# Correlation channels as a fourth term of each convolution product, in place of joins by row group

## The chip, the cores and the metric

The kernel runs on one core of one Trainium2 chip. The metric is the device time of one execution in microseconds (us); before the change the median of three runs is 2604.48 us (2602.58 to 2604.71). Besides, one execution was profiled. In the text PE is the tensor engine, DVE the vector engine, ACT the scalar engine, POOL the GpSimd engine and SP the sync engine, which here issues nearly all DMAs.

## The reference

The input is `x` of 8 images, 768 channels, 32 by 32 pixels, in 32-bit floats. Two layers with a residual follow each other:

```
x = x + attention(groupnorm(x))
x = x + conv(groupnorm(x))
```

The attention has 12 heads of 64 over 1024 tokens. Its scores are made from the variances of v and k alone, `softmax(var_v * var_k^T * scale) @ v`, and a projection by `W_proj` follows.

The second layer is what the change is about:

```
norm   = sqrt(sum(feature**2, channels));  feat_n = feature / max(norm, eps)
corr   = 28 maps: sum over channels of feat_n shifted by (r, c) times feat_n
out    = conv_w @ concat(feature, corr) + conv_b      # a 1x1 convolution, 768 + 28 -> 768
```

So each output value is a sum over 768 feature channels and 28 correlation channels of the same token.

## The kernel before, in words

**Products of seven.** All large matrix products are done by a scheme of Strassen's kind: both operands are cut into two by two blocks, sums of blocks are formed, and seven block products, numbered p = 1 to 7, are added into the four output blocks. For the convolution of one image the output channels are six tiles of 128 (two halves by three groups g = 0 to 2) and the tokens are two halves of 512, so there are 3 x 7 = 21 products, each of three channel tiles of 128. A product is one call chain of `halves` (line 350): every 128 by 512 matmul is issued as two column halves of 64. The products gather in PSUM banks: x for p = 1, 6, 7, 4, y for 5, 3, z for 2 (`BANK`, `FIRST`, `LAST`); x has two buffers, y and z share two. `Wide.take` adds a finished partial sum to the output with DVE.

**Correlation.** `Corr.gram` (line 1151) multiplies windows of the image with turned copies of it, the result is copied out of PSUM into a `win` tile and sent to DRAM, `diagonals`, `scale` and `gather` bring the wanted sums back as rows, and `product` writes them to `cs`: 28 rows, for both token halves and their difference. The weights lie in `wcorr_sb`. Both are tiles of 128 partitions. Four of the seven products, p = 2, 3, 7, 4, are the last of an output block, and the correlation channels are added with those: 12 of the 21 products per image (`Conv.more`).

**Joins.** Before the change `begin` leaves such a product's bank open (`stop=False`); once four or two products are held, `join` (line 1057) issues one matmul of 28 rows by 128 columns for each, the n-th at partitions 32n, so that they use different row groups of the array. For this `wcorr_sb` and `cs` are copied by DMA to partitions 32, 64 and 96. For images 0 to 5 the joins of an image hold 4, 4, 2 and 2 products, for image 6 two each, the last of them at the end of the next projection. When the first join has four, product (0, 2) goes to a bank of its own (`apart`). In the last image the correlation isn't joined to products: `corr` (line 1344) makes 12 products of it alone, by twos on two row groups, and DVE adds them.

**Order of the work.** A planner written out in Python (`Clock`) fixes the order of the instructions of each queue at build time. It has a price for each unit: `T_US` 2.58 for a product, `CORR_US` 1.2 for a join, `STEP_US` 1.73 for an attention step, `EXP` 1.07 for an exponential. `work_off` puts runs of four attention steps of image b (`av`, line 800) between units of the convolution of image b-1, whenever the plan has enough exponentials ahead. A unit waits in the plan for keys such as ("cs", b). `conv_order` gives the order of the 21 products, and with it the order in which SP loads the weight tiles `wt`, seven buffers deep.

**Other places touched.** `keep_warm` issues matmuls of an identity at the start, 31 of them before the first norm (`WARM`). `set_aside` copies three tiles of the features and two of the output before the last projection, with ACT (line 229, tiles `held`), into buffers of the exponentials' pool; the two products that stay over from image 6 use them later. In the last image the turned copies (`turn`) are made by ACT, in other images by POOL; the copies of the gram into `win` are DVE's in all images (line 167 is the helper of all DVE operations).

Of the kernel before, what the change touches and what calls it, by code (L numbers as in the profile page):

```python
# [8 lines left out]
ALU = mybir.AluOpType  # L9
# [43 lines left out]
HELD = 12  # L53
TAIL = 0.0
EXP, SUM, STEP_US = 1.07, 1.15, 1.73
KV_US, T_US, CORR_US = 1.93, 2.58, 1.2
GRAM_US = 1.4
WARM, BRIDGE = 31, (3, 7)

# [12 lines left out]
ORDER = (1, 5, 6, 3, 7, 4, 2)  # L72
QUADS = PAIR[:10] + ((0, 2),) + PAIR[10:12] + ((1, 2), (2, 5), (2, 1)) + SINGLE[2:]
FOUR = P // 4
LOWS = (
# [6 lines left out]
def conv_order(b):  # L82

    return QUADS if b < NB - 2 else (PAIR[:-2] if b == NB - 2 else PAIR) + SINGLE

# [87 lines left out]
def two_layers(ctx, tc, x, wkv, wproj, bproj, wconv, wcorr, bconv, out):  # L173
# [181 lines left out]
    class Banks:  # L355
# [7 lines left out]

        def product(self, g, p, us, width, pairs, taken, home=None):
            self.close(*self.begin(g, p, width, pairs, home=home), us, taken)

        def begin(self, g, p, width, pairs, stop=True, between=None, apart=False, home=None):
            bank = BANK[p]
            if apart:
                t = other([P, width], f"{bank}{g}")  # L370
                for k, (lhsT, rhs) in enumerate(pairs):
                    halves(t, lhsT, rhs, start=k == 0, stop=False, skip_group_check=True)
                return ("apart", g), t
# [12 lines left out]
            clock.pass_time(max(self.free.get(slot, 0.0) - clock.now, 0.0))  # L386
            for k, (lhsT, rhs) in enumerate(pairs):
                halves(
                    t, lhsT, rhs, start=p in FIRST and k == 0, stop=stop and k == len(pairs) - 1, skip_group_check=True
                )  # L390
                if between and k == 0:
                    between()
            return slot, t
# [81 lines left out]
    def load_corr_weights():  # L475

        zero = cs[0:NROW, 0, 0:PAD]
        for r in rows:
            nc.sync.dma_start(out=r[:, 0:PAD], in_=zero)
            nc.sync.dma_start(out=r[:, PAD + N : ROW], in_=zero)  # L480
        for line, step in enumerate(STEP):
            for j in (1, 2, 3):
                n, k = CHANNELS.index(step * j), 3 * line + j - 1
                nc.sync.dma_start(out=wcorr_sb[n : n + 1, :, :], in_=wcorr[k : k + 1, :, :])
                nc.sync.dma_start(out=wcorr_sb[NS + n : NS + n + 1, :, :], in_=wcorr[NS + k : NS + k + 1, :, :])
        nc.sync.dma_start(out=wcorr_sb[2 * NS : NCH, :, :], in_=wcorr[2 * NS : NCH, :, :])
        for n in range(1, 4):
            nc.sync.dma_start(out=wcorr_sb[n * FOUR : n * FOUR + NCH, :, :], in_=wcorr_sb[0:NCH, :, :])

# [447 lines left out]
    class Attention:  # L937
# [32 lines left out]
        def exp_work(self, pair, t):  # L970
# [6 lines left out]
            def job():  # L977
                pair.exponentials(t)
                self.made += 1
                self.exp_at = clock.act  # L980

# [47 lines left out]
    class Wide:  # L1029
        def __init__(self, kind, name, acc, bias, operand, finished, more=None):  # L1030
            self.kind, self.name, self.acc, self.bias = kind, name, acc, bias
            self.operand, self.finished, self.more, self.held = operand, finished, more, []
            self.joined, self.home = [], None

# [3 lines left out]
        def unit(self, g, p, between=None):  # L1038
# [3 lines left out]
            more = self.more(g, p) if self.more else None  # L1042
            if more is None:
                banks.product(g, p, T_US, HF, pairs, taken, self.home if g == 2 else None)
            else:
                apart = (g, p) == (0, 2) and self.joined[:1] == [4]
                self.held.append((*banks.begin(g, p, HF, pairs, stop=False, between=between, apart=apart), taken, *more))
                if len(self.held) == (self.joined[0] if self.joined else 2):
                    self.joined = self.joined[1:]
                    self.join()  # L1050
            t_stream.fill()

        def join(self):

            for n, (slot, t, taken, i, tokens) in enumerate(self.held):
                at = slice(n * FOUR, n * FOUR + NCH)
                nc.tensor.matmul(  # L1057
                    t, lhsT=wcorr_sb[at, i, :], rhs=cs[at, tokens, :], start=False, stop=True, skip_group_check=True
                )
            for slot, t, taken, i, tokens in self.held:  # L1060
                banks.close(slot, t, T_US + CORR_US, taken)
            self.held = []

# [55 lines left out]
    class Corr:  # L1119
# [18 lines left out]
        def gram(self, t):  # L1138
# [22 lines left out]
            def out():  # L1161
                win = wins[t % 2 if t < MT - 1 else 2]
                vector.tensor_copy(win[:, :n], ps[:, :n])
                for side in range(2):
# [58 lines left out]
        def gather(self):  # L1223
# [15 lines left out]
            def product():  # L1239
                vector.tensor_tensor(u, u, v, ALU.mult)  # L1240
                vector.tensor_tensor(cs[0:NCH, 2, :], cs[0:NCH, 0, :], cs[0:NCH, 1, :], ALU.subtract)
                for n in range(1, 4):
                    nc.sync.dma_start(out=cs[n * FOUR : n * FOUR + NCH, :, :], in_=cs[0:NCH, :, :])
                later.after_dve(6.0, lambda: ready.add(("cs", b)))

            later.after(18.0, product)

    class Conv:


        def __init__(self, b, f, acc, after):
            self.b, self.f, self.acc, self.after = b, f, acc, after
            self.early, self.then = False, None
            self.turn = False
            self.apart = [] if b < NB - 1 else [(i, hf) for i in (0, 3, 1, 4, 2, 5) for hf in range(2)]
# [11 lines left out]
        def start(self):  # L1267
# [8 lines left out]
            )  # L1276
            self.wide.joined = [4, 4] if self.b < NB - 2 else []
            ready.add(("acc", self.b))
# [18 lines left out]
        def units(self):  # L1297
            b, held, sizes = self.b, 0, [4, 4] if self.b < NB - 2 else []
            need = {7: (("third", b),), 4: (("fourth", b),)}
            out = []  # L1300
            for g, p in conv_order(b):
                keys, us = need.get(p, ()), T_US
                if self.more(g, p):
                    keys, held = keys + (("cs", b),), held + 1
                    if held == (sizes[0] if sizes else 2):
                        us, held, sizes = us + CORR_US, 0, sizes[1:]
                out.append((us, keys, lambda g=g, p=p: self.unit(g, p)))
# [7 lines left out]
        def set_aside(self):  # L1315

            first, second, third = [expool.tile([P, 2, HF], F32, tag="ex", name=f"held{n}") for n in range(3)]
            self.high = [first[:, 0, :], first[:, 1, :], second[:, 0, :]]
            self.low = {g: third[:, g, :] for g in range(2)}
            for k in range(JH):  # L1320
                act_copy(0.55, self.high[k], self.f[:, JH + k, :HF])
            for g in range(2):
                act_copy(0.55, self.low[g], self.acc[:, g, :HF])

# [7 lines left out]
        def corr_units(self):  # L1332
            return [
                (CORR_US, (("cs", self.b),), lambda n=n: self.corr(self.apart[n : n + 2])) for n in range(0, len(self.apart), 2)
            ]
# [38 lines left out]
    def work_off(rest, attention=None, beside=()):  # L1374
        while rest or (attention and not attention.over()):
            if attention and not attention.over():
                clock.feed_act()
                if attention.can_run():
                    next_to(beside)
                    attention.run()  # L1380
                    next_to(beside)
                    continue
                if ("v", attention.b, 1) in ready and sum(r[0] for r in rest) <= TAIL:
                    clock.pass_time(0.5)
                    continue
# [132 lines left out]
    for b in range(NB + 1):  # L1518
# [8 lines left out]
        if b:  # L1527
# [17 lines left out]
            if b < NB:  # L1545
# [69 lines left out]
```

## Time and profile before

| what | value |
|---|---|
| median of three runs | 2604.48 us |
| the profiled execution | 2601.92 us |
| its span in the profile | 2599.4 us |
| PE busy | 2586.6 us, 14776 instructions |
| DVE busy | 1609.8 us |
| ACT busy | 1368.6 us |
| POOL busy | 416.0 us |
| matmuls from `cs` and `wcorr_sb`, 28x128 form | 192 instructions (84, 42, 42 and 12, 12) |
| DMA copies `cs<-cs` | 24, of 168 KB |

A line of a group reads: source line, engine, operation, output tile and input tiles, shape, count; then busy time, mean ns of one, and idle time before. `128*64` on PE means 128 active rows and 64 active columns. Durations of PE overlap, as matmuls are pipelined, so the pace is read from starts. Every matmul call in 32-bit floats shows as two instructions in the trace.

### The profile page before, as it was taken

The page shows a single profiled execution, that of the slowest core. Times are in us where ns is not written, and L with a number is a line of the kernel's source. Part 1 is how long each engine was busy: PE and PEld are TensorE (multiplying, and loading weights), DVE is VectorE, ACT ScalarE, POOL GpSimd, SP SyncE. Part 2 cuts the span into 40 slices and gives each one's busy share as a digit, 9 for nine tenths or more (in the row PEclk, how much of TensorE's full clock was granted, in tenths as well). Part 3 has the DMA queues.
Part 4 walks back from the last instruction along what each step waited for, and adds up shares of the span by engine and source line. Part 5 has one row for each costly group of instructions (what it writes and reads, how often), then busy time and mean ns, then how long its engine had stood idle before and what let it go on. Part 6 is the DMA issues. An engine that isn't in the chain of part 4 may idle for free.

```text
span 2599.4 us, 40526 instructions
## 1 busy us (share of the span) xinstructions
PE 2586.6 (100%) x14776; PEld 1351.1 (52%) x14776; DVE 1609.8 (62%) x4118; ACT 1368.6 (53%) x1841; POOL 416.0 (16%) x444
## 2 busy tenths in 40 slices
PE   9999999999999999999999999999999999999999
PEld 5654465434664347643476435764356643575333
DVE  6868735775347853488535885357853578535764
ACT  1497179701797017970189701896018960199500
POOL 4320130004300043000330013300133001330000
PEclk9999999999999999999999999999999999999999
DMA  8866366355563655636556365463654636545323
GB/s 295 291 222 216 105 206 206 102 200 168 175 206 96 203 169 173 202 105 200 171 170 201 121 200 169 156 205 118 206 170 144 207 123 205 187 125 169 114 91 106
DMA packets 324716, 448.16 MB, mean 172 GB/s; under 512 B 59810, under 2 KB 245522, under 8 KB 324518
## 3 DMA queue, kind: packets, MB, share of 16 engines
q1 hardware_dynamic: 322454, 442.24, 53.0%
q10 hardware_dynamic: 2064, 3.34, 0.4%
q8 instruction: 117, 1.92, 0.3%
q14 instruction: 81, 0.66, 0.1%
HBM read 376.70 MB, written 64.40 MB: 170 GB/s over the span
## 4 chain that ended last, share of the span: by engine, by line
PE 96%; DVE 1%; DMA 1%; ACT 0%; issue 0%; POOL 0%; SPq 0%; DVEq 0%; ACTq 0%; POOLq 0%
PE x L350 34%; PE av L800 25%; PE y L350 17%; PE z L350 9%; PE own L350 5%; PE gr L1151 3%; PE den L831 1%; PE den L887 1%; PE y L1057 1%; PE z L1057 1%; ACT ex L774 0%; DMA bc<-vdr 0%; DVE acc L167 0%; DMA xn<-in_x_dram 0%; DVE bn L167 0%
## 5 line engine op out<-in xcount | busy, mean ns | idle before, releaser
L774 ACT ACTIVATE ex<-bc,nk 128x1024 f32<-128x1024 f32 x768 | 827.5, 1137 | 403.9 <-DMA bc<-vdr 206.1
L800 PE MATMUL av<-ex,v 128*64 128x512 f32 x3072 | 693.5, 593 | 1.2 <-ACT ex L774 1.1
L800 PEld LDWEIGHTS av<-ex,v 128*64 128x64 f32 x3072 | 332.2, 137 | 318.4 <-issue 199.3
L784 ACT ACTIVATE junk<-bk,vm 128x1024 bf16<-128x1024 f32 x368 | 420.4, 1142 | 28.8 <-DMA bk<-kdr 19.1
L167 DVE TENSOR_TENSOR acc<-acc,ex 128x1024 f32<-128x1024 f32 x300 | 345.2, 1211 | 0.8 <-ACT ex L774 0.8
L229 ACT COPY kp<-x 128x384 f32<-128x384 f32 x28 | 13.3, 478 | 524.1 <-PE x L350 515.4
L350 PE MATMUL y<-kv,s 128*64 128x384 f32 x1488 | 265.3, 487 | 0.3 <-POOL s L636 0.3
L350 PE MATMUL x<-kv,xn 128*64 128x384 f32 x1512 | 259.5, 486 | 0.0
L350 PE MATMUL x<-kv,s 128*64 128x384 f32 x1488 | 256.4, 486 | 0.0
L350 PEld LDWEIGHTS x<-kv,xn 128*64 128x64 f32 x1512 | 139.5, 137 | 104.0 <-issue 83.8
L350 PEld LDWEIGHTS x<-kv,s 128*64 128x64 f32 x1488 | 142.6, 137 | 93.3 <-issue 72.7
L350 PEld LDWEIGHTS y<-kv,s 128*64 128x64 f32 x1488 | 137.0, 137 | 89.9 <-issue 72.4
L530 POOL TENSOR_TENSOR rstda<-vea,neghalf 128x1 f32<-128x1 f32 x8 | 4.8, 595 | 958.6 <-DVE vea L167 958.6
L1136 POOL TENSOR_TENSOR turn<-f,ones 128x384 f32<-128x384 f32 x112 | 110.9, 1010 | 242.7 <-PE gr L1151 165.7
L350 PE MATMUL z<-kv,xn 128*64 128x384 f32 x768 | 133.7, 486 | 0.0
L350 PE MATMUL x<-f,wt 128*64 128x512 f32 x504 | 118.3, 592 | 0.0
L167 DVE TENSOR_TENSOR v<-y,v 128x128 f32<-128x128 f32 x180 | 40.9, 282 | 122.2 <-PE y L350 122.2
L636 POOL TENSOR_TENSOR s<-xn 128x384 f32<-128x384 f32 x64 | 65.6, 1035 | 304.3 <-PE x L350 190.0
L167 DVE BATCH_NORM_STATS2 vbn<-v 128x6 f32<-128x64 f32 x720 | 101.6, 209 | 0.0
L350 PEld LDWEIGHTS z<-kv,xn 128*64 128x64 f32 x768 | 74.9, 137 | 47.3 <-issue 36.6
L167 DVE SCALAR_TENSOR_TENSOR xn<-x,bconv_sb,xn 128x512 f32<-128x512 f32 x63 | 46.3, 745 | 80.8 <-PE x L350 79.7
L1151 PEld LDWEIGHTS gr<-f,turn 128*64 128x64 f32 x1344 | 87.8, 136 | 13.0 <-issue 4.8
(202 smaller groups left out, 3132.3 us busy)
## 6 DMA issues: line engine op xcount, KB each, us to landing
kv<-kvs SPq DMA_DIRECT2D x124, 576.0 KB
kv<-in_wkv_dram SPq DMA_DIRECT2D x95, 576.0 KB
bc<-vdr SPq DMA_DIRECT2D x96, 512.0 KB
f<-in_x_dram SPq DMA_DIRECT2D x48, 512.0 KB
bk<-kdr SPq DMA_DIRECT2D x46, 512.0 KB
x1d<-f SPq DMA_DIRECT2D x42, 512.0 KB
xn<-x1d SPq DMA_DIRECT2D x42, 512.0 KB
out_dram<-xn SPq DMA_DIRECT2D x82, 256.0 KB
```

The source lines that it names most:

```text
L167: return getattr(self.engine, name)(*args, **kw)
L229: nc.scalar.copy(to, at)
L350: nc.tensor.matmul(out[at], lhsT=lhsT[:, at], rhs=rhs, start=start, stop=stop, **kw)
L636: nc.gpsimd.tensor_tensor(self.sums[g][:, 0], a[g][2], a[g][3], ALU.add)
L774: nc.scalar.activation(ex, self.bc[e], AF.Exp, scale=self.kv.nk[self.half][:, h, t : t + 1])
L784: nc.scalar.activation(junk, self.bk[e], AF.Exp, scale=self.kv.m2[self.half][:, h, t : t + 1], accum_out=self.sums[:, e, t : t + 1],)
L800: nc.tensor.matmul(self.av[hf][e * HD : (e + 1) * HD, :], lhsT=self.vt[:, t, e, :], rhs=exs[e][:, hf * HF : (hf + 1) * HF], start=t == 0, ...
L831: nc.tensor.matmul(den[at * 32 : (at + 1) * 32, :], lhsT=ones[:, 0:32], rhs=self.acc[e][:, hf * HF : (hf + 1) * HF], start=True, stop=True,)
L887: nc.tensor.matmul(den[e * HD : (e + 1) * HD, :], lhsT=ones, rhs=self.acc[e][:, at], start=True, stop=True)
L1057: nc.tensor.matmul(t, lhsT=wcorr_sb[at, i, :], rhs=cs[at, tokens, :], start=False, stop=True, skip_group_check=True)
L1136: nc.gpsimd.tensor_tensor(to[:, :, side], half, windows(ones, ones.ap[0], (0, J), (HW, 4), (1, HW)), ALU.mult)
L1151: nc.tensor.matmul(ps[side * HD : (side + 1) * HD, :n].rearrange("p (y x) -> p y x", x=WIDE), lhsT=block[:, j, side, :], rhs=image[:, 4 * ...
```

## The change

The held products and the joins go. A product that takes a correlation term gets a fourth pair, `wcorr_sb` and `cs` on all 128 rows (rows 28 and up are zero), issued by `halves` like the other three, and is closed at once. The copies to partitions 32, 64 and 96 go, and with them the time that the plan allows for them. The 12 separate products of the last image are made in the same form, by fours. The order of the 21 products is one list (`SPACED`) for all images but for the two products that stay over in image 6. `CORR_US` becomes 0.43 and stands for one correlation product. In the last image ACT copies the gram into `win`, and the product that makes `cs` is placed 12 instead of 18 us after its loads. `set_aside` copies with POOL, by a multiplication with ones, at the end of the list of units and after the last exponential. The warm-up has 42 matmuls instead of 31. `TAIL`, which is 0.0, goes with its branch.

```
-WARM, BRIDGE = 31, (3, 7)
+WARM, BRIDGE = 42, (3, 7)
-KV_US, T_US, CORR_US = 1.93, 2.58, 1.2
+KV_US, T_US, CORR_US = 1.93, 2.58, 0.43
-QUADS = PAIR[:10] + ((0, 2),) + PAIR[10:12] + ((1, 2), (2, 5), (2, 1)) + SINGLE[2:]
-FOUR = P // 4
+SPACED = PAIR[:11] + ((0, 2), (2, 1), (1, 4), (2, 5), (2, 6), (2, 3), (1, 2), (2, 7), (2, 2), (2, 4))
...
 def conv_order(b):
-    return QUADS if b < NB - 2 else (PAIR[:-2] if b == NB - 2 else PAIR) + SINGLE
+    return tuple(q for q in SPACED if b != NB - 2 or q not in ((0, 2), (1, 2)))
...
-        for n in range(1, 4):
-            nc.sync.dma_start(out=wcorr_sb[n * FOUR : n * FOUR + NCH, :, :], in_=wcorr_sb[0:NCH, :, :])
...
+                if self.made == HP * MT:
+                    ready.add(("made", self.b))
...
             more = self.more(g, p) if self.more else None
-            if more is None:
-                banks.product(g, p, T_US, HF, pairs, taken, self.home if g == 2 else None)
-            else:
-                apart = (g, p) == (0, 2) and self.joined[:1] == [4]
-                self.held.append((*banks.begin(g, p, HF, pairs, stop=False, between=between, apart=apart), taken, *more))
-                if len(self.held) == (self.joined[0] if self.joined else 2):
-                    self.joined = self.joined[1:]
-                    self.join()
+            us = T_US
+            if more:
+                i, tokens = more
+                pairs.append((wcorr_sb[:, i, :], cs[:, tokens, :]))
+                us += CORR_US
+            banks.product(g, p, us, HF, pairs, taken, between, self.home if g == 2 else None)
             t_stream.fill()
-
-        def join(self):
-            for n, (slot, t, taken, i, tokens) in enumerate(self.held):
-                at = slice(n * FOUR, n * FOUR + NCH)
-                nc.tensor.matmul(
-                    t, lhsT=wcorr_sb[at, i, :], rhs=cs[at, tokens, :], start=False, stop=True, skip_group_check=True
-                )
-            for slot, t, taken, i, tokens in self.held:
-                banks.close(slot, t, T_US + CORR_US, taken)
-            self.held = []
...
-                vector.tensor_copy(win[:, :n], ps[:, :n])
+                if b < NB - 1:
+                    vector.tensor_copy(win[:, :n], ps[:, :n])
+                else:
+                    act_copy(0.3, win[:, :n], ps[:, :n])
...
-                for n in range(1, 4):
-                    nc.sync.dma_start(out=cs[n * FOUR : n * FOUR + NCH, :, :], in_=cs[0:NCH, :, :])
-                later.after_dve(6.0, lambda: ready.add(("cs", b)))
-            later.after(18.0, product)
+                later.after_dve(1.5, lambda: ready.add(("cs", b)))
+            later.after(18.0 if b < NB - 1 else 12.0, product)
...
+            def copy(to, at):
+                one = windows(ones, ones.ap[0], (0, HF // HD), (1, HD))
+                to, at = [a.rearrange("p (n d) -> p n d", d=HD) for a in (to, at)]
+                nc.gpsimd.tensor_tensor(to, at, one, ALU.mult)
             for k in range(JH):
-                act_copy(0.55, self.high[k], self.f[:, JH + k, :HF])
+                copy(self.high[k], self.f[:, JH + k, :HF])
             for g in range(2):
-                act_copy(0.55, self.low[g], self.acc[:, g, :HF])
+                copy(self.low[g], self.acc[:, g, :HF])
...
-            self.turn = not self.turn
-            av = None if self.turn else two_banks(f"av{self.b}_{parts[0][0]}")
-            for n, (i, hf) in enumerate(parts):
-                at = slice(n * FOUR, n * FOUR + NCH)
-                ps = other([P, HF], f"cc{self.b}_{i}_{hf}") if av is None else av[n]
-                nc.tensor.matmul(ps, lhsT=wcorr_sb[at, i, :], rhs=cs[at, hf, :], start=True, stop=True)
-                later.after(1.0, lambda i=i, hf=hf, ps=ps: self.corr_taken(i, hf, ps))
+            some = [other([P, HF], f"cc{self.b}_{i}_{hf}") for i, hf in parts[:2]]
+            for n, (ps, (i, hf)) in enumerate(zip(some + two_banks(f"av{self.b}_{parts[0][0]}"), parts)):
+                halves(ps, wcorr_sb[:, i, :], cs[:, hf, :])
+                later.after((n + 1) * CORR_US + 0.1, lambda i=i, hf=hf, ps=ps: self.corr_taken(i, hf, ps))
...
-                    rest.insert(len(rest) - 3, (0.0, (), conv.set_aside))
+                    rest.append((0.0, (("made", b),), conv.set_aside))
...
-                rest += [first, start] + units[:2] + grams + units[2:18]
-                for n, unit in enumerate(units[18:]):
-                    rest += parts[2 * n : 2 * n + 2] + [unit]
+                rest += [first, start] + units[:2] + grams + units[2:17]
+                for n, unit in enumerate(units[17:]):
+                    rest += parts[n : n + 1] + [unit]
```

More of the change, by code (lines that the diff above doesn't have):

```diff
@@ L53 @@
 HELD = 12
-TAIL = 0.0
 EXP, SUM, STEP_US = 1.07, 1.15, 1.73
-KV_US, T_US, CORR_US = 1.93, 2.58, 1.2
+KV_US, T_US, CORR_US = 1.93, 2.58, 0.43
 GRAM_US = 1.4
-WARM, BRIDGE = 31, (3, 7)
+WARM, BRIDGE = 42, (3, 7)
 BANK = {1: "x", 6: "x", 7: "x", 4: "x", 5: "y", 3: "y", 2: "z"}
@@ L362, in finish, with product, begin @@
                 self.free[slot] = job()
-        def product(self, g, p, us, width, pairs, taken, home=None):
-            self.close(*self.begin(g, p, width, pairs, home=home), us, taken)
-        def begin(self, g, p, width, pairs, stop=True, between=None, apart=False, home=None):
+        def product(self, g, p, us, width, pairs, taken, between=None, home=None):
+            self.close(*self.begin(g, p, width, pairs, between, home), us, taken)
+        def begin(self, g, p, width, pairs, between=None, home=None):
             bank = BANK[p]
[L369 to L373, printed above, removed]
             of = "x" if bank == "x" else "y"
@@ L388, in begin @@
                 halves(
-                    t, lhsT, rhs, start=p in FIRST and k == 0, stop=stop and k == len(pairs) - 1, skip_group_check=True
+                    t, lhsT, rhs, start=p in FIRST and k == 0, stop=k == len(pairs) - 1, skip_group_check=True
                 )
@@ L1031, in __init__ @@
             self.kind, self.name, self.acc, self.bias = kind, name, acc, bias
-            self.operand, self.finished, self.more, self.held = operand, finished, more, []
-            self.joined, self.home = [], None
+            self.operand, self.finished, self.more, self.home = operand, finished, more, None
         def place(self, i, hf):
@@ L1253, in __init__ @@
             self.early, self.then = False, None
-            self.turn = False
             self.apart = [] if b < NB - 1 else [(i, hf) for i in (0, 3, 1, 4, 2, 5) for hf in range(2)]
@@ L1276, in start @@
             )
-            self.wide.joined = [4, 4] if self.b < NB - 2 else []
             ready.add(("acc", self.b))
@@ L1297, in units @@
         def units(self):
-            b, held, sizes = self.b, 0, [4, 4] if self.b < NB - 2 else []
+            b = self.b
             need = {7: (("third", b),), 4: (("fourth", b),)}
@@ L1303, in units @@
                 if self.more(g, p):
-                    keys, held = keys + (("cs", b),), held + 1
-                    if held == (sizes[0] if sizes else 2):
-                        us, held, sizes = us + CORR_US, 0, sizes[1:]
+                    keys, us = keys + (("cs", b),), us + CORR_US
                 out.append((us, keys, lambda g=g, p=p: self.unit(g, p)))
@@ L1333, in corr_units @@
             return [
-                (CORR_US, (("cs", self.b),), lambda n=n: self.corr(self.apart[n : n + 2])) for n in range(0, len(self.apart), 2)
+                (4 * CORR_US, (("cs", self.b),), lambda n=n: self.corr(self.apart[n : n + 4]))
+                for n in range(0, len(self.apart), 4)
             ]
         def corr(self, parts):
-            self.turn = not self.turn
-            av = None if self.turn else two_banks(f"av{self.b}_{parts[0][0]}")
-            for n, (i, hf) in enumerate(parts):
-                at = slice(n * FOUR, n * FOUR + NCH)
-                ps = other([P, HF], f"cc{self.b}_{i}_{hf}") if av is None else av[n]
-                nc.tensor.matmul(ps, lhsT=wcorr_sb[at, i, :], rhs=cs[at, hf, :], start=True, stop=True)
-                later.after(1.0, lambda i=i, hf=hf, ps=ps: self.corr_taken(i, hf, ps))
+            some = [other([P, HF], f"cc{self.b}_{i}_{hf}") for i, hf in parts[:2]]
+            for n, (ps, (i, hf)) in enumerate(zip(some + two_banks(f"av{self.b}_{parts[0][0]}"), parts)):
+                halves(ps, wcorr_sb[:, i, :], cs[:, hf, :])
+                later.after((n + 1) * CORR_US + 0.1, lambda i=i, hf=hf, ps=ps: self.corr_taken(i, hf, ps))
         def corr_taken(self, i, hf, ps):
@@ L1381, in work_off @@
                     next_to(beside)
-                    continue
-                if ("v", attention.b, 1) in ready and sum(r[0] for r in rest) <= TAIL:
-                    clock.pass_time(0.5)
                     continue
```

## The prediction

> **What bounds the kernel now.** I read the first page of the profile first, then the waits of PE, then the order of time on PE. Three lines of the page (span, busy time by engine, the chain that ended last):
>
> ```profile
> span 2599.4 us, 40526 instructions
> PE 2586.6 (100%) x14776; PEld 1351.1 (52%) x14776; DVE 1609.8 (62%) x4118; ACT 1368.6 (53%) x1841; POOL 416.0 (16%) x444
> PE x L350 34%; PE av L800 25%; PE y L350 17%; PE z L350 9%; PE own L350 5%; PE gr L1151 3%; PE den L831 1%; PE den L887 1%; PE y L1057 1%; PE z L1057 1%; ACT ex L774 0%; DMA bc<-vdr 0%; DVE acc L167 0%; DMA xn<-in_x_dram 0%; DVE bn L167 0%
> ```
>
> PE is busy for all but 12.8 us, and the chain is PE for 96%. A busy PE need not run at its peak, so I asked what it waits for. The complete list of PE's waits has only these of any size:
>
> ```profile
> PE pma L350 <- DVE mva L167: 2.8, 1, 2.8
> PE gr L1151 <- DVE win L167: 2.0, 4, 1.0
> PE warm L419 <- POOL ident masks.py:199: 1.6, 1, 1.6
> PE av L800 <- ACT ex L774: 1.1, 3, 0.6
> ```
>
> So nothing that the change does on DVE, ACT, POOL or the DMA queues can win much; what it does to the number and form of PE's instructions counts in full. The granted clock is 1.00 in every stretch that I asked for. One stretch of PE in order of time (start, duration, then line, tiles, shape, count), in the convolution of the first image:
>
> ```profile
> 441.22 5.47 PE L350 MATMUL y<-t1f,wt 128*64 128x512 f32 x24
> 446.37 5.47 PE L350 MATMUL x<-t2f,wt 128*64 128x512 f32 x24
> ...
> 473.20 2.90 PE L350 MATMUL y<-f,wt 128*64 128x512 f32 x12
> 476.03 0.69 PE L1057 MATMUL y<-cs,wcorr_sb 28*128 28x512 f32 x1
> 476.04 0.70 PE L1057 MATMUL x<-cs,wcorr_sb 28*128 28x512 f32 x2
> 476.05 1.10 PE L1057 MATMUL y<-cs,wcorr_sb 28*128 28x512 f32 x2
> 476.57 0.59 PE L1057 MATMUL x<-cs,wcorr_sb 28*128 28x512 f32 x2
> 476.58 0.59 PE L1057 MATMUL y<-cs,wcorr_sb 28*128 28x512 f32 x1
> 477.10 1.06 PE L831 MATMUL den<-acc,ones 128*32 128x512 f32 x8
> ```
>
> Starts tell the true pace, since durations overlap. Each matmul call is two instructions in the trace. Twenty-four instructions of the 128x64 form take 446.37 - 441.22 = 5.15 us: 0.2146 each, 0.858 us for one call of `halves` (two column halves, four instructions), 2.575 us for a product of three. A join of four products is the eight instructions at 476.03: the four row groups start within 20 ns of each other and run side by side. From 473.20 the product should end at 475.775; the next work starts at 477.10, so this join costs 1.33 us for four products.
>
> **The change, part by part.**
>
> *The correlation as a fourth pair of each product.* Per image there are 12 products that take a correlation term (p = 2, 3, 7, 4 by three groups), so 96 in eight images. The two programs' instruction lists agree: 96 calls of 28x128 form go (192 instructions, lines 1057 and 1344), 192 calls of 128x64 form come (384 instructions, in `halves`). No other PE work changes but 11 warm-up calls. Added: 96 x 0.858 = 82.4 us. The nearest rows are those of the same shape; the quickest pace is 0.2146 a instruction, the slowest group of L350 at 128x512 has 0.2256 with its waits, so the ends are 82.4 and 86.6. I take 82.4.
>
> *The joins go.* I measured all 33 places as above (next start, less start of the last product, less 2.575). Twelve joins of four cost 15.8 us (1.33 each, one 1.17), eighteen joins of two cost 21.0 us (1.16 mostly, 1.31 where the next tile follows differently), the three groups of four at L1344 in the last image 2.56, 2.07 and 2.07, together 6.7. Sum 43.4 us. Eight joins stand before `den` products of line 831, whose 128x32 form brings a switch of its own (the last start before it is 0.523 us ahead instead of 0.422), which stays: 0 to 0.8 us comes back, I take 0.5. So PE's own work grows by 82.4 - 43.4 + 0.5 = 39.5.
>
> *A rule beside the row.* The rows show four row groups in 1.07 us from first start to the next work, where four full-height products will need 3.43. The Trainium skill, "TensorEngine Tiling (Array Packing)", section Overview, gives a contraction of at most 32 rows an up to fourfold gain from packing, which speaks against undoing the packing; its section Key Properties adds that a change of the tiling mode drains the engine. By full packing without any drain each join would be one pass of 0.858 (an estimate from that page), the old cost 36 x 0.858 = 30.9 us and the loss 51.5; the trace's 1.16 to 1.33 includes what the switch costs, and the sum goes by it.
>
> *Copies and waits ahead of the joins.* 27 DMAs (`cs<-cs` 24, `wcorr_sb` 3) go, and `cs` counts as ready 1.5 us instead of 6.0 us after its product. They cost SP about 0.83 us of issue each, off the path; PE nowhere waits for `cs` (largest in the waits: 0.2 us at a weight load). Worth 0; at most that 0.2.
>
> *The other order of products.* The same 21 products. What could cost is a bank used again before DVE took it: in the new order three places have one product between two uses of a bank, (0,4) to (2,1), (2,5) to (2,3), (2,7) to (2,4). One product is 2.575 us, with a correlation 3.43; a take is 0.69 to 0.75 us on DVE. The old order even has (2,6) straight behind (2,1) in one bank, and PE's list has no wait on it. Worth 0 while DVE's queue holds less than 1.7 us of other work; beyond that see rival B.
>
> *The planner's price.* CORR_US 0.43 is half of the 0.858 a product takes, so PE comes 5 us behind the plan per image. DVE, ACT and SP are then early against PE, not late; 0. If something placed too early blocks its queue, it is rival B again.
>
> *Warm-up.* 11 more calls before the first norm. In order of time the warm calls start 0.111 us apart per instruction from 5.4 us on, so 22 add 2.45 us; PE waits 2.83 us there for `mva`. Hidden; 0, and at most 0.2 if that gap shrinks.
>
> *Aside copies from ACT to POOL, last attention.* ACT and PE in order of time:
>
> ```profile
> 2440.86 1.65 ACT L229 COPY held<-f 128x512 f32<-128x512 f32 x3
> 2447.36 1.14 ACT L229 COPY held<-xn 128x512 f32<-128x512 f32 x2 [4.85 <-PE av L800]
> 2448.40 4.51 ACT L774 ACTIVATE ex<-bc,nk 128x1024 f32<-128x1024 f32 x4
> ...
> 2445.44 3.60 PE L800 MATMUL av<-ex,v 128*64 128x512 f32 x16
> 2449.60 3.15 PE L800 MATMUL av<-ex,v 128*64 128x512 f32 x10 [0.56 <-ACT ex L774]
> 2452.97 1.50 PE L800 MATMUL av<-ex,v 128*64 128x512 f32 x5 [0.22 <-ACT ex L774]
> ```
>
> The copies of `held<-xn` wait 4.85 us on ACT for a buffer, four exponentials stand behind them, and PE starves. From 2445.44 PE has 32 instructions of av (6.87), a product (2.575) and a join (1.16), so 2456.0; it gets to the next work at 2458.46: 2.4 us lost. With the copies on POOL and behind the last exponential, this goes: 0 to -2.4, I take -2.1, since the page shows nothing else late there. On POOL each copy is about 1.35 us (1010 ns for 384 columns, scaled), five are 6.7. Queued behind them on POOL is only the next norm's `rstdb`, 60 us later. On SP the reload of `f` columns 3 to 5 (first at 2458) must wait for them, with weight loads behind it; seven weight tiles are ahead, 18 us of PE. 0; without that cover some 2 us.
>
> *Last image's gram copied by ACT.* The four waits of the second list, here in place:
>
> ```profile
> 2529.94 1.58 PE L1151 MATMUL gr<-f_last,turn 128*64 128x133 f32 x24 [0.98 <-DVE win L167]
> 2531.95 2.94 PE L1151 MATMUL gr<-f_last,turn 128*64 128x133 f32 x48 [0.43 <-DVE win L167]
> 2535.12 2.94 PE L1151 MATMUL gr<-f_last,turn 128*64 128x133 f32 x48 [0.23 <-DVE win L167]
> 2538.44 1.01 PE L1151 MATMUL gr<-f_last,turn 128*64 128x76 f32 x24 [0.38 <-DVE win L167]
> ```
>
> DVE's copies queued there behind 0.6 us operations. On ACT a gram brings two turns (0.93) and a copy of about 0.3, so 1.25 us against 1.45 of PE. But a turn now stands behind a copy that waits for PE and for the DMA that empties the window. -2.0 to +2; I take -1.3.
>
> *The correlation product 6 us sooner in the last image.* It is placed 12 us after its loads are begun, not 18. Those issues ran 2561.3 to 2566.2, so they have 7 us to land; the product ran at 2576.6. The first corr unit is also one product earlier. PE did not wait there; 0. At the tail the last two units are the same two, and the 3.9 us from PE's last start to the end stay.
>
> **Sum.** +39.0 +0.5 (den switches) -2.1 -1.3 = +36.1 us. Against the profiled execution's own 2601.92 us (span 2599.4 and 2.5 around it) that is 2638.0. That execution lies 2.6 us under the median of the three timed runs, 2604.48, which gives 2640.6; I forecast 2640.5, +1.4%.
>
> **The rivals.**
>
> A. *ACT becomes the bound of the grams*: a turn held up by window copies, about 1.0 us for each of 8 grams instead of the gain: +36.1 +1.3 +8 = +45, 2650. For it: the window copies of DVE did wait for the DMA (1.0 to 1.6 us, four times). Against: 1.25 against 1.45 us.
>
> B. *Banks or blocked queues make PE wait*: three places per image in seven images, each for one sum of DVE's attention work (1.16 us) = 24: 2665. For it: those sums come in pairs and fours on DVE. Against: no such wait in the old order, which has a closer pair.
>
> C. *The other side, faster*: a correlation product costs what the planner says, 0.43 us: 41.3 - 43.4 + 0.5 - 3.4 = -5, 2599.5. For it: only that constant. Against: every row of that shape, av included, stands at 0.858. It decides below (43.4 + 2.9) / 96 = 0.48 us a product.
>
> D. *The joins cost more than their place shows*, since four banks held open and four takes at once press DVE: another 6 us back, 2634. For it: DVE waits 88 us for joins. Against: PE's list has no wait for a take.
>
> **How the numbers follow.** The forecast's own terms end at 34.6 (43.4 off 82.4, no switch, both gains whole) and 46.2 (86.6 less 43.4, 0.8, no gain, 2 lost in the grams): 2639 to 2651. Forecast 0.78, D 0.06, A 0.06, B 0.06, C 0.02, and 0.02 that it is some lesser mix near no change. The range 2631 to 2651 holds the forecast, A, and D with the 2 to 3 us by which runs differ; left out are C, B's full price and the mix. Within 0.2% (5.2 us, about what a measurement of this kernel can tell from no change) 0.01; faster 0.02; slower 0.97.
>
> **What would show it.** Right: PE busy time up by some 35 to 37 us with the share still 100%; groups with `cs,wcorr_sb` at 128*64, 384 instructions of about 593 ns, 12 products an image, each 3.43 us from start to start; no 28-row form; no `PE av <- ACT ex` in the last attention; the DVE `win` waits gone or replaced by ACT `win`. Wrong: new waits of PE on DVE `xn` (B) or on ACT `turn` or `win` (A), or a start-to-start time of a cs group well under 0.8 us (C).

## The result, and the profile after

The changed kernel takes 2641.43 us (median of four runs, 2639.12 to 2644.45) against 2603.53 us for the kernel before (median of four, 2601.29 to 2604.71; three of them are the runs told of ahead): a ratio of 1.0148, 95% interval 1.0136 to 1.0160. It is slower by 38 us. The forecast was 2640.5. The four runs of the changed kernel lie in two pairs, 2639.1 and 2639.4 us at a mean granted clock of 1.00 and 2643.4 and 2644.5 at 0.999; the profile is of the first.

The page of the changed kernel, the lines that answer to those of before:

```profile
span 2637.4 us, 40929 instructions
PE 2628.9 (100%) x14990; PEld 1380.6 (52%) x14990; DVE 1612.0 (61%) x4110; ACT 1370.3 (52%) x1844; POOL 427.1 (16%) x449
```

The span grew by 38.0 us, PE's busy time by 42.3 (its idle time fell from 12.8 to 8.5), and DVE, ACT and POOL hardly moved (2.2, 1.7 and 11.1 us). PE is still the bound; it only has more to do. Its waits, the largest:

```profile
PE warm L412 <- POOL ident masks.py:199: 1.6, 1, 1.6
PE av L791 <- ACT ex L765: 1.3, 2, 1.1
PE gr L1130 <- POOL turn L1115: 0.5, 2, 0.2
PE ct L351 <- DVE ir L165: 0.4, 1, 0.4
PE gr L1130 <- ACT win L227: 0.4, 2, 0.2
```

No wait for `mva` and none for DVE's `win` are left, and there is none on a take of DVE. The wait of `av` for `ex` is there, but at another place than before (below). PE in order of time, two products of the convolution of image 6:

```profile
2480.19 2.75 PE L348 MATMUL z<-f,wt 128*64 128x512 f32 x12
2482.77 1.03 PE L348 MATMUL z<-cs,wcorr_sb 128*64 128x512 f32 x4
2483.62 7.04 PE L791 MATMUL av<-ex,v 128*64 128x512 f32 x32
2490.49 2.75 PE L348 MATMUL x<-t4f,wt 128*64 128x512 f32 x12
2493.07 1.03 PE L348 MATMUL x<-cs,wcorr_sb 128*64 128x512 f32 x4
```

From 2480.19 to 2483.62 it is 3.43 us for a product with its correlation, 2.58 of it for the three feature tiles and 0.85 for the fourth. There is no gap between the two.

To see where the 38 us lie I cut both traces at the same places: the first matmul of each image's second norm (`pmb`), the first and the last gram of the last image, and the end.

| stretch | before, us | after, us | difference |
|---|---|---|---|
| start to norm of image 0 | 329.1 | 328.9 | -0.2 |
| to image 1 | 269.5 | 277.1 | +7.6 |
| to images 2 to 6, together | 1601.2 | 1628.9 | +27.7 |
| to image 7 (its attention) | 317.1 | 318.2 | +1.1 |
| to the first gram of image 7 | 9.2 | 9.4 | +0.2 |
| the grams of image 7 | 13.2 | 11.2 | -2.0 |
| to the end | 60.2 | 63.7 | +3.5 |

A middle image loses 5.54 us on average (27.7 over five): 12 x 0.858 = 10.30 for the products, less 4.76 for its four joins, a figure that the next section works out. The last stretch loses 10.3 less 6.7.

### The profile page after: what moved, and what is told of

Read it like the earlier page. It is cut to its first block, busy times and chain, and to the rows that moved or that the text cites. A ratio compares the mean times of both kernels' runs of the same rounds, so it can differ in the third digit from the quotient of the medians.

```text
span 2637.4 us, 40929 instructions
## 1 busy us (share of the span) xinstructions
PE 2628.9 (100%) x14990; PEld 1380.6 (52%) x14990; DVE 1612.0 (61%) x4110; ACT 1370.3 (52%) x1844; POOL 427.1 (16%) x449
## 4 chain that ended last, share of the span: by engine, by line
PE 97%; DMA 1%; ACT 1%; DVE 0%; issue 0%; SPq 0%; POOL 0%; ACTq 0%; POOLq 0%; DVEq 0%
PE x L348 35%; PE av L791 24%; PE y L348 17%; PE z L348 10%; PE own L348 5%; PE gr L1130 3%; PE den L822 1%; ACT ex L765 1%; PE warm L412 1%; PE den L878 1%; DMA bk<-kdr 0%; ACT junk L775 0%; DMA vdr<-rsv 0%; DVE acc L165 0%; PE av L348 0%
```

## The experiments

**The correlation's matmuls left out, from the kernel before and from the changed one.** If the loss lies in these matmuls alone, the two kernels without them must be equally fast.

```
 # e1, from the kernel before: products are closed as they are, joins issue nothing
-                self.held.append((*banks.begin(g, p, HF, pairs, stop=False, between=between, apart=apart), taken, *more))
+                self.held.append((*banks.begin(g, p, HF, pairs, between=between, apart=apart), taken, *more))
...
-                nc.tensor.matmul(
-                    t, lhsT=wcorr_sb[at, i, :], rhs=cs[at, tokens, :], start=False, stop=True, skip_group_check=True
-                )
+                pass
...
 # e2, from the changed kernel
-                pairs.append((wcorr_sb[:, i, :], cs[:, tokens, :]))
...
```

In both, the last image's separate products go too, and with them the additions of DVE that took their results.

> The kernel before with every matmul of the correlation left out (the joins and the separate products of the last image; the correlation does not reach the output), the order of all else kept. Main theory, prices read from starts on PE: 43.4 us less than before, about 2560 us. Rival, a join is one packed pass of 0.858 and the rest of its place is something that stays: 30.9 us less, 2573. Rival D (open banks press DVE besides): 6 us beyond the 43.4, 2554.

> The changed kernel with every correlation product left out (the correlation does not reach the output). Main theory, 0.858 us a product: 82.4 us less than the changed kernel, 2559 us, and so 1 to 4 us under the kernel before without its joins. Rival C (0.43 us a product): 2600. If new waits hold part of the loss (rival B), they stay and the time is above 2563.

Measured: 2566.64 us (2565.97 to 2568.46) from the kernel before, ratio 0.9861 (0.9845 to 0.9878); 2564.66 us (2564.45 to 2566.61) from the changed one, ratio to the kernel before 0.9854 (0.9839 to 0.9869). The kernel before took 2602.86 us beside these runs and the two kinds that follow. So 36.2 us go with the joins and 76.8 us with the products. The two remainders are 2 us apart, and that is all that is left of a difference of 38: the loss is in these matmuls. Rival C is out; by it the second would have been 2600.

Both drops fall short of the sums, 43.4 and 82.4. In the last stretch, where PE alone sets the pace, they are exact: 55.7 to 49.0 (6.7) and 59.3 to 49.0 (10.3) from the last gram to the last matmul. In the middle images I laid each pair of traces side by side, operation by operation. Each of the 12 products shows as a step of 0.86 us; then one run of `av` and the next product give 0.85 back, since PE comes sooner and is held there. The four joins show as steps of 1.33, 1.11, 1.16 and 1.16, that is 4.76 and not 4.97: a join that stands before a `den` product of line 822 or 831 hides 0.21 us of switch that `den` has anyhow. In the five middle images without joins PE also has one new wait each, of 0.2 to 1.9 us, at the first products of the next projection (`x<-v,wt`); they come to 3.8 us, of the some 4.6 by which these images fall short of five times 4.76. So the prices at the place hold; leaving the work out showed less than its price here, because new waits took the place of some of it.

**The joins issued twice.**

```
+            for last in (False, True):
                 for n, (slot, t, taken, i, tokens) in enumerate(self.held):
                     at = slice(n * FOUR, n * FOUR + NCH)
                     nc.tensor.matmul(
-                        t, lhsT=wcorr_sb[at, i, :], rhs=cs[at, tokens, :], start=False, stop=True, skip_group_check=True
+                        t, lhsT=wcorr_sb[at, i, :], rhs=cs[at, tokens, :], start=False, stop=last, skip_group_check=True
                     )
```

> The kernel before with the matmuls of each of the 30 joins issued twice in a row (the correlation counts twice in images 0 to 6). If a join is a pass and a switch of form, the second pass costs a pass alone, 0.86 to 0.91 us: 26 to 27 us more, 2630. If a join's price goes by its matmuls with no fixed part, the second costs what the first does, 36.7 us: 2640.

Measured 2627.52 us (2625.32 to 2629.38), ratio 1.0094 (1.0078 to 1.0109): 24.7 us more for 30 joins, 0.82 each; a middle image grows by 3.5 us on average, 0.87 a join. One join in order of time, first of the kernel before, then doubled:

```profile
1742.92 0.69 PE L1057 MATMUL y<-cs,wcorr_sb 28*128 28x512 f32 x1
...
1743.48 0.59 PE L1057 MATMUL y<-cs,wcorr_sb 28*128 28x512 f32 x1
1744.00 2.79 PE L350 MATMUL z<-f,wt 128*64 128x512 f32 x12
```

```profile
1757.70 0.69 PE L1058 MATMUL y<-cs,wcorr_sb 28*128 28x512 f32 x1
...
1759.12 0.59 PE L1058 MATMUL y<-cs,wcorr_sb 28*128 28x512 f32 x1
1759.63 2.79 PE L350 MATMUL z<-f,wt 128*64 128x512 f32 x12
```

1.08 us from the first start to the next work, 1.93 with the second pass. A pass of four row groups is therefore 0.85 us, the same as one product by column halves, and a join of 1.33 is a pass and some 0.47 us for the change of form to and fro. Joins of two, mostly 1.16, leave 0.30; the difference lies ahead of the join, where 0.10 us pass instead of 0.25. That settles why the change loses: one pass served four products, or two, and now each has its own.

**The changed kernel on 28 rows.** The fourth pair takes only the 28 rows that are not zero.

```
-                pairs.append((wcorr_sb[:, i, :], cs[:, tokens, :]))
+                pairs.append((wcorr_sb[0:NCH, i, :], cs[0:NCH, tokens, :]))
```

(and the same in the last image's products)

> The changed kernel with its correlation products on 28 rows instead of 128, still by column halves. Main theory: the time of a product is set by the columns streamed, not by rows, so each stays at 0.858 us, and only a switch of form is added, 0 to 0.45 us each way of 96: 2641 to 2680. If rows set the time, 28 of 128 save up to 64 us: 2577.

Measured 2668.28 us (2667.41 to 2669.31), ratio to the kernel before 1.0251 (1.0235 to 1.0266), 27 us more than on 128 rows. In order of time:

```profile
1802.31 2.94 PE L348 MATMUL z<-f,wt 128*64 128x512 f32 x12
1805.18 1.07 PE L348 MATMUL z<-cs,wcorr_sb 28*64 28x512 f32 x4
1806.19 2.80 PE L348 MATMUL x<-f,wt 128*64 128x512 f32 x12
```

3.88 us from product to product here, where 128 rows take 3.43; over a whole middle image, 329.1 us against 325.7, the difference is smaller, 0.28 us for each of its 12 products. Fewer rows save nothing, and the change of form is paid. That it is the change and not the 28 rows shows in the last image, where four such products follow each other: inside that run, pairs of instructions start 0.43 us apart, as on 128 rows, while 0.52 us instead of 0.42 pass ahead of its first. Some 5 of the 27 us are not the form's but a lower clock near the end (last section). Filling the rows with zeros, as the change does, is the better of these two.

**The parts in the last image, alone and together, on the kernel before.** The edits are those of the change: `set_aside` by POOL at the end of the units, and `act_copy` for `win` in the last image.

> The kernel before with the aside copies on POOL behind the last exponential and nothing else. Main theory: 2.1 to 2.4 us less, 2601.3 us, and no wait of av for ex in the last attention. Rival: the reload of f waits for POOL and holds up weights, so nothing or a loss of some 2 us, 2605.

> The kernel before with the last image's gram copied by ACT and nothing else. Main theory: 1.3 to 2.0 us less, 2602 us, with the 2.0 us of waits on win reduced. Rival A: turns stand behind the copies, PE waits on turn or win, up to 8 us more.

> The kernel before with two of the change's parts alone: the aside copies on POOL behind the last exponential, and the last image's gram copied by ACT. Prediction's terms: 2.1 and 1.3 us less, 2600.0 us, both starved stretches gone from PE. Rival A (ACT bounds the grams): +8 us there, about 2610.

| kernel | median, us | ratio to before, 95% interval | its stretch in the trace |
|---|---|---|---|
| aside copies by POOL | 2600.89 | 0.9995 (0.9986 to 1.0004) | attention of image 7: 317.07 to 314.64 |
| gram copied by ACT | 2600.70 | 0.9991 (0.9982 to 1.0000) | grams of image 7: 13.2 to 11.2 |
| both | 2598.25 | 0.9982 (0.9973 to 0.9991) | 314.6 and 11.2 |

The intervals of the single ones reach 1; the traces show each gain at its place, 2.4 and 2.0 us, and both together are told apart from the kernel before. In the last attention the run of `av` that the prediction showed broken by waits is now one piece (kernel with both parts):

```profile
2443.65 7.09 PE L800 MATMUL av<-ex,v 128*64 128x512 f32 x32
2450.57 2.74 PE L350 MATMUL z<-f,wt 128*64 128x512 f32 x12
```

Rival A is out: the grams with ACT's copies run with waits of 0.2 us.

**The plan's price and the order of the products,** on the changed kernel.

```
 # e4
-KV_US, T_US, CORR_US = 1.93, 2.58, 0.43
+KV_US, T_US, CORR_US = 1.93, 2.58, 0.86
 # e7
-    return tuple(q for q in SPACED if b != NB - 2 or q not in ((0, 2), (1, 2)))
+    return (PAIR[:-2] if b == NB - 2 else PAIR) + SINGLE
```

> The changed kernel with the plan's price of a correlation product at 0.86 us, what the trace shows, instead of 0.43. Main theory, PE's work sets the time and the plan's error costs nothing: within 2 us of the changed kernel, 2641, at most the 1.3 us of waits on the exponentials less. If the false price had cost waits (rival B), several us less, under 2636.

> The changed kernel with the 21 products in the order that image 7 had before, pairs first and then the singles, in all images. Main theory, the order costs nothing while PE never waits for a bank: 2641, within 2 us. If the spread order was worth something, PE waits for takes at the end of the list, where (2, 6) follows (2, 5) and (2, 1) at one product's distance: up to 24 us more, 2665.

Measured: 2639.17 us (2638.20 to 2640.24) with the true price, ratio 1.0138 (1.0124 to 1.0152); 2641.32 us (2639.86 to 2644.32) with the old order, ratio 1.0148 (1.0134 to 1.0162). Neither is told apart from the changed kernel by its interval; the kernel with the true price took what the changed kernel's two runs at a clock of 1.00 took, 2639.1 and 2639.4. In the traces a middle image takes 325.7 us in both, to a tenth as in the changed kernel. The first convolution's stretch differs: 277.1 us in the changed kernel, 276.8 with the true price and 280.8 in the old order, where `av` waits 4.6 us for `ex` (1.5 at 352 us and 3.0 at 466 us). But that profile is of the slowest of the four runs by 2.5 us, so one trace doesn't show that the order costs this in general. Price and order thus cost nothing in the steady images, and rival B has no case there; what the order does at the first convolution stays open.

**Row groups kept and used more.** If a pass for four costs what a pass for one does, the last image's 12 separate products, which use two row groups, should use four. I added this to the two parts above.

```
-            self.turn = not self.turn
-            av = None if self.turn else two_banks(f"av{self.b}_{parts[0][0]}")
-            for n, (i, hf) in enumerate(parts):
+            some = [other([P, HF], f"cc{self.b}_{i}_{hf}") for i, hf in parts[:2]]
+            some += two_banks(f"av{self.b}_{parts[0][0]}")
+            for n, (ps, (i, hf)) in enumerate(zip(some, parts)):
                 at = slice(n * FOUR, n * FOUR + NCH)
-                ps = other([P, HF], f"cc{self.b}_{i}_{hf}") if av is None else av[n]
...
 # e8 besides: image 6 joins [4] first; e9 instead: cs after 12.0 us in the last image; e10: e9 with WARM 42
```

> The kernel before with the two parts above, and more of its correlation by four row groups at once: the last image's 12 products in three groups of four on four row groups, and image 6's first four in one join. By the prices of the joins (1.33 for four, 1.16 for two; 6.7 us for the last image's three groups now): 3.4 less from the parts, 6.7 - 4.0 = 2.7 and 2.4 - 1.3 = 1.0 less from the fours: 2603.5 - 7.1 = 2596.4 us. If four banks taken at once by DVE near the end hold up the last outputs, up to 2 us of it are lost.

Measured 2599.78 us (2598.10 to 2601.51), ratio 0.9986 (0.9977 to 0.9995): no better than the two parts alone (2598.25). In the last image PE stands at the first group:

```profile
2582.09 1.64 PE L1353 MATMUL cc<-cs,wcorr_sb 28*128 28x512 f32 x4
2583.55 2.07 PE L1353 MATMUL av<-cs,wcorr_sb 28*128 28x512 f32 x4
2585.55 2.79 PE L350 MATMUL x<-t,wt 128*64 128x512 f32 x12
```

3.46 us instead of 1.07 as in its second and third group. The weight loads' lines say why, idle in brackets:

```profile
2582.61 0.29 PEld L1353 LDWEIGHTS cc<-cs,wcorr_sb 28*128 28x128 f32 x2 [0.23 <-DMA cs<-cs]
2583.55 0.29 PEld L1353 LDWEIGHTS av<-cs,wcorr_sb 28*128 28x128 f32 x2 [0.65 <-DMA cs<-cs]
2584.50 0.29 PEld L1353 LDWEIGHTS av<-cs,wcorr_sb 28*128 28x128 f32 x2 [0.66 <-DMA cs<-cs]
```

The copies of `cs` to the second, third and fourth group landed too late. And image 7's attention stretch took 316.7 us, not 314.6: with the larger join in image 6, PE waits for takes and sums of DVE (0.8, 0.6 and 0.5 us). So the next two kernels leave image 6 alone and make `cs` sooner, as the change does.

> The kernel before with the two last-image parts (aside copies on POOL, gram copied by ACT), its correlation in the last image by four row groups at once, and there cs made 12 instead of 18 us after its loads, so that the copies to all row groups have landed; image 6 keeps joins of two. By the joins' prices 6.7 - 4.0 = 2.7 us less than the two parts alone (2598.3): 2595.6. If the copies still land late, PE waits some 2 us at the first group, 2597.6.

> The same with 42 warm-up matmuls instead of 31, the change's last part. As predicted (the gap of PE before the first norm only gets filled): no change, 2595.6. New theory, from two profiles in which PE runs at half pace for some 9 us after that gap of 2.1 to 2.8 us and loses 3.1 us: the filled gap keeps the pace in every execution, so the median falls by 0.5 to 2 us against the kernel with 31, and its first product starts near 16.3 us.

Measured: 2596.68 us (2594.94 to 2599.90, 10 runs), ratio 0.9976 (0.9967 to 0.9985), and with 42 warm-up matmuls 2594.16 us (2592.89 to 2595.01, 5 runs), ratio 0.9964 (0.9951 to 0.9978). From the last gram to the last matmul it is 52.7 us in both, 3.0 less than before. The second is the fastest of this study: 8.4 us under the kernel before (2602.54 beside it) and about 47 under the changed one. What the warm-up does is told in the last section.

## Why the prediction was right, and where its terms were off

The direction and the size rested on two prices read from starts on PE, and both held. That 2640.5 lies within 1 us of the median is in part luck: slips of the small terms cancel (below), and the median lies between two pairs of runs some 4.5 us apart.

- *Added products, 82.4 us.* 0.858 each, as forecast: the steps of 0.86 between the traces, and 10.3 us for twelve in the last stretch. The upper end, 86.6, rested on a misreading: 0.2256 us an instruction is the figure of `av` (693.5 us for 3072), while groups of line 350 go up to 0.239 (`y<-f,wt`, 60.3 us for 252). It did not come into play.
- *Joins, 43.4 us.* Their places are right; what goes with them is a little less. The term for `den` was too small: 0.21 us in the middle image that I laid side by side, so about 1.7 us at eight such places (an estimate), not the 0.5 taken and more than the 0.8 allowed. That is +1.2 on the sum.
- *The rule weighed beside it.* The Trainium skill, "TensorEngine Tiling (Array Packing)", section Key Properties, has the array drained when the tiling mode changes; the doubled joins agree, with some 0.47 us for the two changes around a join of four. The fourfold gain of its section Overview was reached only on the pass itself: 1.33 us against 3.43 is 2.6 times.
- *Aside copies on POOL, -2.1.* The stretch alone shows -2.4, what the rows had given. *Gram by ACT, -1.3.* It shows -2.0: I had taken two thirds of a gain that came whole, in fear of rival A.
- *Copies and waits, order, price: 0.* Held in the steady images. The price and the order were each tried alone, the copies to the other partitions were not.
- *Missed: the first convolution's stretch,* +7.6 where the products less the joins give some 5.8. Of the rest, 1.1 us is a new wait of `av` for `ex` at 461 us: ACT has four passes of the denominators before the exponentials that PE wants; the run of `av` now begins 2.0 us earlier, at 454.63 instead of 456.67, and those exponentials 1.3 us later, at 460.03 instead of 458.75. The wait stays with the true price (1.0) and is 3.0 in the one trace of the old order. The remaining 0.7 us say little: in seven profiles of kernels that do the same work in it, the kernel before among them, this stretch took 269.2 to 271.1 us. I did not take this apart further.
- *Missed: the warm-up, 0.* In the profiled execution it was so (-0.2). Over the runs of e9 and e10 it was not (last section).
- *Missed: PE's busy time.* Up by 42.3 us, not by 35 to 37: the waits for `mva` and `win`, which the prediction itself saw go, had been idle time, and 4.3 us of idle became busy.

In one sum, against the span's 38.0: 39.0 + 1.7 - 2.4 - 2.0 - 0.2 + 1.8 = 37.9, where the forecast had 36.1. The slips are +1.2 and +1.8 against -1.2; they partly cancel. Rival D asked for relief on DVE beyond the joins' places, more than 43.4 us; the kernel without joins won only 36.2 us and showed new waits instead, so it has no support.

## What to carry to other kernels

On an engine that is busy throughout, price an edit by the starts of its instructions, form by form, and count instructions in the program; here two prices gave a loss of 38 us to within 2 us. A matmul of few rows cost a whole pass over its columns here, 0.86 us on 28 rows as on 128: let several share one pass on row groups, and weigh the saved passes against the change of form before and after. When work is left out to measure its price, look in the trace for the waits that take its place, or the price comes out too low, as here with 36.2 us for 43.4 and 76.8 for 82.4.

## What the runs showed of the hardware that I had not expected

**PE's clock can drop behind a gap shorter than one that left it alone.** With 31 warm-up matmuls PE is idle ahead of the first norm. In the profile of the kernel before the gap was the longest, 2.83 us, and the clock stayed; in three other profiles of kernels with 31 the wait was 1.8 to 2.2 us and the clock fell. In four more it was 2.3 to 2.6 us and the clock stayed at 1.00. The kernel e8 in windows of time and in order of time:

```profile
0.00:10.00 10.00, 8.36 (x54) 8.37 (x55) 5.06 (x9) 0.00 (x0) 4.65 (x18) 1.00 0.83 288
10.00:20.00 10.00, 7.79 (x42) 6.46 (x42) 6.78 (x17) 4.56 (x6) 1.55 (x2) 0.66 1.03 382
20.00:30.00 10.00, 10.00 (x64) 4.36 (x62) 9.86 (x16) 2.64 (x7) 10.00 (x7) 1.00 0.59 233
```

```profile
13.29 0.38 PE L350 MATMUL pma<-mva,group 128*64 128x1 f32 x4 [2.21 <-DVE mva L167]
15.48 3.35 PE L419 MATMUL warm<-ident 128*128 128x128 f32 x14
18.77 4.71 PE L350 MATMUL x<-kv,xn 128*64 128x384 f32 x24
```

The same places in the kernel before, and then in e10 with 42 warm-up matmuls:

```profile
13.45 0.28 PE L350 MATMUL pma<-mva,group 128*64 128x1 f32 x4 [2.83 <-DVE mva L167]
14.74 1.83 PE L419 MATMUL warm<-ident 128*128 128x128 f32 x14
```

```profile
13.35 0.28 PE L350 MATMUL pma<-mva,group 128*64 128x1 f32 x4 [0.24 <-DVE mva L167]
14.63 1.83 PE L419 MATMUL warm<-ident 128*128 128x128 f32 x14
```

The third figure from the right of a window is the granted clock, 0.66 in the second. Fourteen warm instructions took 3.35 us there and 1.83 us in the kernel before, and the stretch to image 0's norm took 332.6 us instead of 329.1. The trace's own record of the clock gives 0.5 for 6.83 us in e8 and in the kernel with the aside copies alone, for 3.41 us in e9, and none there in the kernel before; the expectation of e10 had put the slow stretch at some 9 us and the gaps of its two profiles at 2.1 to 2.8 us, where they were 2.1 and 2.2. In all six profiles of kernels with 42 matmuls the gap is 0.2 us or none and the clock stays at 1.00 there.

The runs of e9 and e10, which differ in nothing else, fit this. Eight of e9's ten have a mean clock of 0.999 and a median span of 2594.0 us; its other two and all five of e10 have 1.00, with spans of 2592.2 and 2592.2 and a median of 2592.4. So 1.6 of the 2.5 us between the two kernels go with the clock; the rest lies outside of the span and is not explained. The 42 matmuls are no guarantee, however: the changed kernel has them too, and two of its four runs are at 0.999 and took 4 to 5 us longer. Of these two there is no trace, so where the clock fell in them is not known.

The Trainium skill, "TensorE: Matmul & The Clock Gate", tells of a free-running window of 3.41 us (section "What's actually happening") and advises against idle gaps of more than about 3 us (section "Why this matters for your kernels"); the lengths of the drops agree with such a window, but here the clock fell behind gaps of 1.8 to 2.2 us and stayed behind one of 2.83 us. What decides between them was not tried.

**A second drop without a gap.** In the kernel on 28 rows the clock fell near the end, 0.79 from 2640 to 2666 us, with PE at work; the record gives 0.5 for 6.83 and then 3.41 us. The changed kernel, whose last products differ only in the rows, has 1.00 there in its profile. By these lengths the drop cost up to 5.1 us (an estimate, half of 10.24), most of the 5.8 us by which that stretch is longer. What brought it about was not tried.
